# A decoder layer on one Trainium2 core: the last two tiles written out as one ordered piece, routers in pairs, contexts loaded ahead

## The chip, the cores and the metric

The kernel runs on one core of a Trainium2 chip. The metric is the device time of one execution in microseconds (us), the median of several runs. The core's engines are named as in the profile: PE (TensorE, matmuls; PEld its weight loads), DVE (VectorE), ACT (ScalarE), POOL (GpSimd) and SP (SyncE, which here issues DMAs; ACT issues some too).

## What is computed

One decoder layer in float32 on 32 sequences of 64 tokens, 512 features each, so 2048 tokens or 16 tiles of 128 tokens (two sequences a tile):

```python
x = x + attention(layernorm(x))        # 32 heads of 128, q and k rms-normed
x = x + cross(layernorm(x), ctx)       # per sequence, over features
x = x + experts(layernorm(x))

def cross(up, down):                   # up: 64 x 512, down: 64 x 128
    q, k, v = Wq @ up, Wk @ down, Wv @ down
    return Wskip @ up + (softmax(q.T @ k / 8) @ v.T).T

def experts(h):                        # 64 experts, the best 8 of each token
    s = softmax(h @ router.T + router_bias)
    w = s where s is among the token's 8 largest, else 0
    return h * sum(w) + w @ expert_bias
```

The change concerns only the second and the third line.

## The kernel before

**Stages.** Until about 1396 us the kernel does the self-attention of all 16 tiles. Then comes the output stage: the output projection, a 2048 by 4096 by 512 product by Strassen's scheme with seven products for each pair of tiles (`strassen_out`, line 974 and after; `chunks`, matmuls on L879). When a tile's sum with the residual is whole, `done(t, x)` starts its tail: the generator `after_attention`, which does the cross attention and then the experts. Each `yield n` in it gives PE back to the projection: the main loop (end of `decoder_layer`) calls `advance()` after every four matmuls of a product, and `n` is how many calls the tail sits out. So the tails of pair p run between the products of pair p+1, and the tails of the last pair (tiles 14 and 15) have little or nothing to hide behind.

**What sets the order.** PE's order is the program's (`manual_schedule` for PE in the whole kernel). In the output stage the other engines' orders are chosen by the framework's scheduler, which follows the dependences and the buffers; each engine then runs its list strictly in order. Buffers come from pools: PSUM has three banks `ps_s` (kv, energies, logits), two `ps_t` (transposes), three `ps_a` (projection, mixtures, experts). DMAs of a queue are issued in order; each also waits on one of eight semaphores, dealt out in turn among all queues, until the DMA that had it before has landed.

**Cross attention of a tile** (L1084 to L1158). The context `ct` (128x128) is loaded on SP's queue (L1090) when the tail starts. Layernorm: statistics on DVE, `rstd` on POOL (L259, L260) or, in tiles with `name.endswith("15")`, on ACT (L262, L263), the normalising on DVE (L269). `kv`: two matmuls (L1094, L1095), copied by ACT (L1098). Energies `e`: eight matmuls on 64 rows each (L1105). The skip product `py_x` (L1114); softmax on DVE and ACT (L1123 to L1139); eight transposes `pt_x` (L279), two ACT copies `att` (L1144); the mixture of two matmuls on 64 columns each into `py_x` (L1149); the sum on DVE (L1158).

**Experts of a tile** (L1162 to L1226). Layernorm again, four transposes `pt_f` (L279), ACT copy `ft` (L1168), router `pl_f`: four matmuls with `ft` as weights and the router's 64 columns moving (L1173). Bias, the eight largest, softmax, mask and share `wds` on DVE and ACT (L1178 to L1205). The shares are transposed (`pw_f`, L1212) and copied (L1214), for two tiles at once up to tile 13, and each tile's product with the experts' biases (`pm_f`, 512 columns, L1222) is added (L1225) and stored (L1226, 256 KB).

**Fillers.** At the end, where PE has gaps, `fill_behind` puts dummy transposes (`fill`, L230) after named steps of tiles 14 and 15, 76 in all.

Of the kernel before, what the change touches and what calls it, by code (L numbers as in the profile page):

```python
# [13 lines left out]
P = 128  # L14
# [21 lines left out]
def _bc(ap, n):  # L36

    return ap.unsqueeze(2).to_broadcast([ap.shape[0], ap.shape[1], n])
# [3 lines left out]
def decoder_layer(  # L42
# [172 lines left out]
    def load(to, what):  # L215

        tc.keep_in_program_order(nc.sync.dma_start(out=to, in_=what))
# [7 lines left out]
    def fill(count):  # L225
# [3 lines left out]
        for _ in range(count):  # L229
            nc.tensor.transpose(filled[0], ident, ident)  # L230


    FILL = {
        (NT - 1, "keys"): 18,
        (NT - 2, "mixtures"): 18,
        (NT - 1, "probabilities"): 6,
        (NT - 2, "router's input"): 5,
        (NT - 2, "router"): 10,
        (NT - 1, "router's input"): 5,
        (NT - 1, "router"): 3,  # L240
        (NT - 2, "weights"): 3,
        (NT - 2, "experts"): 8,
    }

    def fill_behind(t, what):
        if (t, what) in FILL:
            fill(FILL[t, what])

    def statistics(xs, name, on_gpsimd=False):

        n = len(xs)
# [12 lines left out]
        return [(mv[:, i, 0:1], rstd[:, i : i + 1]) for i in range(n)]  # L264

    def layernorm(xt, name):
        ((mean, rstd),) = statistics([xt], name, not name.endswith(str(NT - 1)))
        xn = work.tile([P, D], F32, tag="xn", name=f"xn_{name}", bufs=3)
        nc.vector.tensor_scalar(xn, xt, mean, rstd, ALU.subtract, ALU.mult)  # L269
        return xn  # L270
# [810 lines left out]
        done(ta, xa)  # L1081
        done(tb, xb)

    def cross_attention(t, xt, apart):  # L1084

        name = f"x{t}"
        ct = work.tile([P, MCTX], F32, tag="ct", name=f"ct_{t}")
        nc.sync.dma_start(out=ct, in_=ctx_flat[bass.ts(t, P), :])  # L1090
        xn = layernorm(xt, name)
        yield 1
        kv = ps_s.tile([P, 2, MCTX], F32, tag="ps", name=f"kv_{t}")
        nc.tensor.matmul(kv[:, 0, :], wqk, ct, start=True, stop=True)  # L1094
        nc.tensor.matmul(kv[:, 1, :], ct, xw[:, 2, :], start=True, stop=True)  # L1095

        kvs = work.tile([P, 2, MCTX], F32, tag="kvs", name=f"kvs_{t}")
        nc.scalar.copy(kvs, kv)  # L1098
        fill_behind(t, "keys")
        yield apart  # L1100
        halves = [slice(b * SEQ, (b + 1) * SEQ) for b in range(2)]
        e = [ps_s.tile([P, 4, MCTX], F32, tag="ps", name=f"e{b}_{name}") for b in range(2)]
        for c in range(4):
            for b, half in enumerate(halves):
                nc.tensor.matmul(  # L1105
# [3 lines left out]
                    start=True,  # L1109
                    stop=True,  # L1110
                )
        def skip():
            py = ps_a.tile([P, D], F32, tag="pa", name=f"py_{name}")
            nc.tensor.matmul(py, xw[:, 3, :], xn, start=True, stop=False, skip_group_check=True)  # L1114
            return py


        py = skip() if t == NT - 1 else None
        probs = []
        for b in range(2):  # L1120

            mx = small.tile([P, 4], F32, tag="mx4", name=f"mx{b}_{name}")
            nc.vector.tensor_reduce(mx, e[b], AX.X, ALU.max)  # L1123
            neg = small.tile([P, 4], F32, tag="neg4", name=f"neg{b}_{name}")
            nc.vector.tensor_scalar(neg, mx, -(SEQ**-0.5), None, ALU.mult)
            prob = work.tile([P, 4, P], F32, tag="probx", name=f"prob{b}_{name}", bufs=3)
            sums = small.tile([P, 4], F32, tag="sums4", name=f"sums{b}_{name}")
            for c in range(4):
                nc.scalar.activation(
                    prob[:, c, :],  # L1130
                    e[b][:, c, :],
                    AF.Exp,
                    bias=neg[:, c : c + 1],
                    scale=SEQ**-0.5,
                    accum_out=sums[:, c : c + 1],
                )
            inv = small.tile([P, 4], F32, tag="inv4", name=f"inv{b}_{name}")
            nc.vector.reciprocal(inv, sums)
            nc.vector.tensor_tensor(prob, prob, _bc(inv, P), ALU.mult)  # L1139
            probs.append(prob)  # L1140
        yield 5
        att = work.tile([P, 2, 4, P], F32, tag="att", name=f"att_{name}", bufs=1)
        for b in range(2):
            nc.scalar.copy(att[:, b, :, :], transposed(probs[b], f"{name}_{b}"))  # L1144
        fill_behind(t, "probabilities")
        yield 2
        py = py or skip()
        for b, half in enumerate(halves):
            nc.tensor.matmul(  # L1149
                py[half, :],  # L1150
                kvs[:, 1, half],
                att[:, b, :, :].rearrange("m c n -> m (c n)"),
                start=False,
                stop=b == 1,
                skip_group_check=True,
            )
        fill_behind(t, "mixtures")
        nc.vector.tensor_tensor(xt, xt, py, ALU.add)  # L1158

    chosen_by = {}  # L1160

    def experts(t, xt):  # L1162
        name = f"f{t}"
        xn = layernorm(xt, name)

        yield 8 if t == NT - 2 else 3
        ft = work.tile([P, KC, P], F32, tag="ft", name=f"ft_{name}", bufs=1)
        nc.scalar.copy(ft, transposed(xn.rearrange("p (kc k) -> p kc k", k=P), name))  # L1168
        fill_behind(t, "router's input")
        yield 1  # L1170
        pl = ps_s.tile([P, NEXP], F32, tag="ps", name=f"pl_{name}")
        for kc in range(KC):
            nc.tensor.matmul(  # L1173
                pl, ft[:, kc, :], rwt[:, kc, :], start=kc == 0, stop=kc == KC - 1
            )
        fill_behind(t, "router")
        lg = work.tile([P, NEXP], F32, tag="lg", name=f"lg_{name}")
        nc.vector.tensor_tensor(lg, pl, rb_b, ALU.add)  # L1178
        top = small.tile([P, 8], F32, tag="top", name=f"top_{name}")
        nc.vector.max(top, lg)  # L1180
        neg = small.tile([P, 1], F32, tag="neg", name=f"neg_{name}")
        nc.vector.tensor_scalar(neg, top[:, 0:1], -1.0, None, ALU.mult)
        ex = work.tile([P, NEXP], F32, tag="ex", name=f"ex_{name}")
        den = small.tile([P, 1], F32, tag="den", name=f"den_{name}")
        nc.scalar.activation(ex, lg, AF.Exp, bias=neg, accum_out=den)
        inv = small.tile([P, 1], F32, tag="inv1", name=f"inv1_{name}")
        nc.vector.reciprocal(inv, den)

        rest = work.tile([P, NEXP], F32, tag="rest", name=f"rest_{name}")
        nc.vector.match_replace(rest, top, lg, -3e38)  # L1190
        chosen = work.tile([P, NEXP], F32, tag="chosen", name=f"chosen_{name}")
        nc.vector.tensor_tensor(chosen, lg, rest, ALU.not_equal)

        alone = t >= NT - 2
        side = 0 if alone else t % 2
        if side:
            wds, other = chosen_by.pop(t - 1)
        else:
            wds = work.tile([P, 2, NEXP], F32, tag="wds", name=f"wds_{name}")
        wd = wds[:, side, :]  # L1200
        nc.vector.scalar_tensor_tensor(wd, ex, inv, chosen, ALU.mult, ALU.mult)
        ws = small.tile([P, 1], F32, tag="ws", name=f"ws_{name}")
        nc.vector.tensor_reduce(ws, wd, AX.X, ALU.add)

        nc.vector.scalar_tensor_tensor(xt, xn, ws, xt, ALU.mult, ALU.add)  # L1205
        if not alone and not side:
            chosen_by[t] = wds, xt
            return
        yield 3
        n = NEXP if alone else 2 * NEXP  # L1210
        pw = ps_t.tile([P, P], F32, tag="pt", name=f"pw_{name}")
        nc.tensor.transpose(pw[0:n, :], wds.rearrange("p a e -> p (a e)")[:, 0:n], ident)  # L1212
        wt = work.tile([P, P], F32, tag="wt", name=f"wt_{name}")
        nc.scalar.copy(wt[0:n, :], pw[0:n, :])  # L1214
        fill_behind(t, "weights")
        yield 1

        both = [(t, xt)] if alone else [(t - 1, other), (t, xt)]
        pms = [ps_a.tile([P, D], F32, tag="pa", name=f"pm{i}_{name}") for i in range(len(both))]
        for i, pm in enumerate(pms):  # L1220
            rows = slice(i * NEXP, (i + 1) * NEXP)
            nc.tensor.matmul(pm, wt[rows, :], eb_sb[rows, :], start=True, stop=True)  # L1222
        fill_behind(t, "experts")
        for (at, it), pm in zip(both, pms):
            nc.vector.tensor_tensor(it, it, pm, ALU.add)  # L1225
            nc.sync.dma_start(out=out_flat[bass.ts(at, P), :], in_=it)  # L1226

    def after_attention(t, xt):
        second = t % 2 and t < NT - 1
        if second:  # L1230
            yield 0
        yield from cross_attention(t, xt, 3 if second else 1)
        yield from experts(t, xt)


    phase = ExitStack()
# [314 lines left out]
    work = ctx.enter_context(tc.tile_pool(name="output", bufs=2, reuse_waits="tile"))  # L1551
    bo_b = work.tile([P, D], F32, tag="bo", name="bo_b", bufs=1)
    load(bo_b, bo.partition_broadcast(P))
    outs = {1: strassen_out(1, right, start_tail, a12)}
    next(outs[1])

# [34 lines left out]
                advance()  # L1591
    while tails:
        advance()


# [49 lines left out]
```

## Time and profile before

| what | us |
|---|---|
| median of 3 runs (lowest, highest) | 1869.87 (1869.63, 1870.72) |
| profiled execution, own time | 1869.75 |
| its span, first to last instruction | 1868.0 |
| granted PE clock over the span | 0.999 |
| PE busy, 1400 to 1480 | 77.07 of 80 |
| PE busy, 1480 to 1780 | 300.00 of 300 |
| PE busy, 1780 to 1841 | 60.36 of 61 |
| PE busy, 1841 to 1868 (fillers included) | 22.30 of 27 |

Times in the trace are counted from the span's first instruction. A line of a timeline has start, duration, engine, line of code, operation, output and inputs, shapes, count, and in brackets the idle time ahead of it with what ended it. A line of waits has the waiting instruction, what it waited for, and the total, number and longest of these waits. A float32 matmul shows as two records (`x2`), a transpose as one. A record's duration reaches beyond the start of the next one, since matmuls are pipelined: what a group costs PE is the distance from its start to the next group's.

### The profile page before, as it was taken

The page shows a single profiled execution, that of the slowest core. Times are in us where ns is not written, and L with a number is a line of the kernel's source. Part 1 is how long each engine was busy: PE and PEld are TensorE (multiplying, and loading weights), DVE is VectorE, ACT ScalarE, POOL GpSimd, SP SyncE. Part 2 cuts the span into 40 slices and gives each one's busy share as a digit, 9 for nine tenths or more (in the row PEclk, how much of TensorE's full clock was granted, in tenths as well). Part 3 has the DMA queues.
Part 4 walks back from the last instruction along what each step waited for, and adds up shares of the span by engine and source line. Part 5 has one row for each costly group of instructions (what it writes and reads, how often), then busy time and mean ns, then how long its engine had stood idle before and what let it go on. Part 6 is the DMA issues. An engine that isn't in the chain of part 4 may idle for free.

```text
span 1868.0 us, 40676 instructions
## 1 busy us (share of the span) xinstructions
PE 1850.4 (99%) x16914; PEld 1616.9 (87%) x16914; DVE 1245.1 (67%) x2110; ACT 653.6 (35%) x1577; POOL 1014.7 (54%) x852
## 2 busy tenths in 40 slices
PE   9999999999999999999999999999999999999999
PEld 8888998898899888898889988988888888788876
DVE  6877777777666758777667767766684445554555
ACT  2344444444433443434443343444312202221222
POOL 4866777776667639776667777766242121212120
PEclk9999999999999999999999999999999999999999
DMA  4234434433443343333343333334944231223100
GB/s 143 69 122 144 134 125 131 131 109 110 131 136 114 114 139 112 109 109 103 130 134 123 109 110 114 103 115 141 312 122 159 91 116 68 71 94 116 46 26 23
DMA packets 164650, 215.06 MB, mean 115 GB/s; under 512 B 10161, under 2 KB 135153, under 8 KB 160369
## 3 DMA queue, kind: packets, MB, share of 16 engines
q1 hardware_dynamic: 157648, 206.62, 34.2%
q10 hardware_dynamic: 6816, 5.83, 1.0%
q8 instruction: 133, 2.18, 0.5%
q14 instruction: 53, 0.43, 0.1%
HBM read 172.05 MB, written 40.37 MB: 114 GB/s over the span
## 4 chain that ended last, share of the span: by engine, by line
PE 88%; DVE 4%; DMA 3%; POOL 3%; ACT 1%; issue 1%; SPq 0%; ACTq 0%; POOLq 0%; DVEq 0%
PE p_w L685 32%; PE py L879 17%; PE va L417 11%; PE vb L417 8%; PE o L622 3%; PE s L585 3%; PE ms_w L821 3%; PE pt_p L279 1%; PE pa L475 1%; PE e_x L1105 1%; PE py_x L1149 1%; PE pt_x L279 1%; POOL w L120 1%; PE pl_f L1173 1%; PE py_x L1114 1%; PE pb L475 1%
## 5 line engine op out<-in xcount | busy, mean ns | idle before, releaser
L685 PE MATMUL p_w<-x,w 128*128 128x256 f32 x2940 | 721.1, 382 | 2.5 <-DVE qk L696 1.7
L685 PEld LDWEIGHTS p_w<-x,w 128*128 128x128 f32 x2940 | 521.4, 190 | 59.3 <-DVE qk L696 1.2
L417 PEld LDWEIGHTS va<-w,x 128*128 128x128 f32 x2048 | 268.6, 192 | 13.0
L696 DVE TENSOR_TENSOR qk<-p_w,qk 128x512 f32<-128x512 f32 x360 | 213.1, 599 | 94.6 <-PE p_w L685 92.3
L433 ACT COPY v<-va 128x256 f32<-128x256 f32 x256 | 96.2, 376 | 497.5 <-PE va L417 497.5
L417 PE MATMUL va<-w,x 128*128 128x128 f32 x2048 | 269.9, 275 | 0.0
L709 DVE TENSOR_TENSOR qk<-p_w,qk 128x512 f32<-128x512 f32 x360 | 220.5, 620 | 46.5 <-PE p_w L685 43.1
L120 POOL TENSOR_TENSOR w<-w 128x768 f32<-128x768 f32 x126 | 249.7, 1993 | 2.4
L572 POOL TENSOR_TENSOR qk<-qk,rs 128x512 f32<-128x512 f32 x128 | 173.0, 1352 | 111.8 <-DMA rs<-row_w 99.4
L295 POOL TENSOR_TENSOR prob<-prob,inv 128x512 f32<-128x512 f32 x64 | 79.2, 1237 | 281.5 <-DVE inv L294 278.3
L879 PE MATMUL py<-wo,a 128*128 128x256 f32 x992 | 227.2, 382 | 0.0
L386 ACT ACTIVATE sq<-qk 128x512 f32<-128x512 f32 x256 | 161.4, 631 | 183.6 <-DVE qk L709 64.4
L879 PEld LDWEIGHTS py<-wo,a 128*128 128x128 f32 x992 | 184.1, 190 | 32.9 <-issue 8.6
L417 PEld LDWEIGHTS vb<-w,x 128*128 128x128 f32 x1536 | 201.3, 192 | 9.7
L417 PE MATMUL vb<-w,x 128*128 128x128 f32 x1536 | 202.4, 275 | 0.0
L574 DVE SCALAR_TENSOR_TENSOR qk<-qk,gqk,rs 128x512 f32<-128x512 f32 x128 | 164.7, 1287 | 3.8 <-DMA rs<-row_w 3.5
L879 PE MATMUL py<-wo_t,a 128*128 128x256 f32 x672 | 155.1, 382 | 0.0
L879 PEld LDWEIGHTS py<-wo_t,a 128*128 128x128 f32 x672 | 124.3, 190 | 18.2 <-issue 1.6
L1003 POOL TENSOR_TENSOR x<-x,p 128x256 f32<-128x256 f32 x42 | 42.9, 1043 | 166.7 <-ACT p L1056 72.2
L437 DVE TENSOR_TENSOR v<-vb,v 128x256 f32<-128x256 f32 x192 | 80.9, 421 | 57.0 <-ACT v L433 28.8
L765 POOL TENSOR_TENSOR qk<-qk 128x256 f32<-128x256 f32 x120 | 102.8, 857 | 10.5 <-DVE qk L709 5.8
L287 DVE TENSOR_REDUCE mx<-s 128x8 f32<-128x512 f32 x64 | 44.1, 689 | 85.4 <-PE s L585 85.3
(197 smaller groups left out, 2253.7 us busy)
## 6 DMA issues: line engine op xcount, KB each, us to landing
rs<-row_w SPq DMA_DIRECT2D x120, 512.0 KB
mixed<-ot SPq DMA_DIRECT2D x64, 512.0 KB
a<-mixed SPq DMA_DIRECT2D x32, 1024.0 KB
w<-in_wq_dram SPq DMA_DIRECT2D x64, 256.0 KB
w<-in_wk_dram SPq DMA_DIRECT2D x62, 256.0 KB
w<-in_wv_dram SPq DMA_DIRECT2D x62, 256.0 KB
x<-in_x_dram SPq DMA_DIRECT2D x20, 256.0 KB
rs<-row SPq DMA_DIRECT2D x8, 512.0 KB
```

The lines of the kernel that those rows point to most:

```text
L120: on.tensor_tensor(*(it.rearrange("p c j d -> p (c j) d") for it in (out, a, b)), ALU.subtract)
L386: nc.scalar.activation(sq, of, AF.Square)
L417: nc.tensor.matmul(to[:, j, :], left[i][:, c, j, :], right[i][:, c, 2, :], start=first and j == 0 and c == 0, stop=c == 1, skip_group_chec ...
L433: nc.scalar.copy(self.v[h, ab], what)
L437: nc.vector.tensor_tensor(it, what, it, ALU.add)
L572: nc.gpsimd.tensor_tensor(k, k, rk, ALU.mult)
L574: lambda: nc.vector.scalar_tensor_tensor(q, q, gqk, rq, ALU.mult, ALU.mult)
L685: nc.tensor.matmul(bank[:, s, :], self.w.inner[o][i], inner_x[self.half, o][i], start=first and s == 0, stop=True, skip_group_check=True,)
L696: nc.vector.tensor_tensor(to(t, j), bank, add(t, j), ALU.add)
L709: nc.vector.tensor_tensor(to(t, j), bank, to(t, j), ALU.add)
L765: on.tensor_tensor(to, to, what, ALU.add)
L879: nc.tensor.matmul(py, a[:, g, :], b[g // KH][:, g % KH, :], start=n == 0 and g == 0, stop=n == last and g == NHG - 1,)
```

## The change

**Contexts.** `context(t)` issues the load; those of tiles 0 and 1 are issued when the output stage's pool opens, ahead of `strassen_out(1, ...)` and so ahead of three of its loads on SP's queue; on that queue these loads now also have other semaphores of the eight.

**Rstd.** `layernorm` takes POOL except for tile 13's cross attention (`name != f"x{NT - 3}"`), which takes ACT.

**Routers in pairs**, tiles 0 to 13. The first tile of a pair only fills its half of `fts`. With the second tile, the router's weights are the stationary side and both tiles' features move, the result being logits by token across; ACT copies it, PE turns it back, and the shares of both tiles are worked out one after the other. The last steps come where they came before.

```diff
+        plt = ps_s.tile([P, P], F32, tag="ps", name=f"plt_{name}")
         for kc in range(KC):
-            nc.tensor.matmul(
-                pl, ft[:, kc, :], rwt[:, kc, :], start=kc == 0, stop=kc == KC - 1
-            )
+            for side in range(2):
+                nc.tensor.matmul(
+                    plt[side * NEXP : (side + 1) * NEXP, :],
+                    rwt[:, kc, :],
+                    fts[:, side, kc, :],
+                    start=kc == 0,
+                    stop=kc == KC - 1,
+                )
+        lgt = work.tile([P, P], F32, tag="wt", name=f"lgt_{name}")
+        nc.scalar.copy(lgt, plt)
+        yield 0
+        pl = ps_s.tile([P, 2, NEXP], F32, tag="ps", name=f"pl_{name}")
+        nc.tensor.transpose(pl.rearrange("p a e -> p (a e)"), lgt, ident)
...
+        for side, (at, x_, xn_) in enumerate(tiles):
...
+        yield 2
```

**The last two tiles.** Tile 14's cross attention stops after its probabilities; tile 15's tail only loads its context. `FILL` goes. When all else is recorded, `last_two()` does the rest of both tiles in one order, given by hand on PE, DVE, ACT and POOL (cut; `normed`, `router`, `shares`, `turned_shares` are as the steps before, except that `shares` leaves the division by `den` to the last addition, and `neg` of the softmax is on ACT):

```diff
+        norm_b, xn_b, *_ = normed(xb, b, False)
+        norm_b()
+        kvs_b = keys(NT - 1, ct_b)
+        py_a = skip(NT - 2, xn_a)
+        mix_in(py_a, kvs_a, att_a)
+        nc.vector.tensor_tensor(xa, xa, py_a, ALU.add)
+        norm_a, xn_a, *_ = normed(xa, f"f{NT - 2}", True)
+        e = energies(NT - 1, xn_b, kvs_b)
+        py_b = skip(NT - 1, xn_b)
+        pc = ps_s.tile([P, NEXP], F32, tag="ps", name="pc")
+        for kc in range(KC):
+            nc.tensor.matmul(pc, mean_of, rwt[:, kc, :], start=kc == 0, stop=kc == KC - 1)
...
+        norm_a()
+        nc.vector.tensor_tensor(
+            centred, rwt, pc.unsqueeze(1).to_broadcast([P, KC, NEXP]), ALU.subtract
+        )
...
+        pt_a = turned_4(xn_a, f"f{NT - 2}")
+        fill(9)
+        probabilities(0)
...
+        nc.vector.tensor_copy(ft_a, pt_a)
+        pl_a = router(ft_a, rwt, f"f{NT - 2}")
+        probabilities(1)
+        lg_a = work.tile([P, 2, NEXP], F32, tag="lg", name=f"lg_{a}")[:, 0, :]
+        nc.vector.tensor_tensor(lg_a, pl_a, rb_b, ALU.add)
+        wd_a, ws_a, inv_a = shares(lg_a, f"f{NT - 2}")
+        fill(6)
+        mix_in(py_b, kvs_b, att_b)
+        nc.vector.tensor_tensor(xb, xb, py_b, ALU.add)
+        wt_a = turned_shares(wd_a, f"f{NT - 2}")
+        fill(5)
+        pt_b = turned_4(xb, f"f{NT - 1}")
...
+        nc.scalar.copy(ft_b, pt_b)
+        norm_b, xn_b, rstd, mean = normed(xb, f"f{NT - 1}", False)
+        nc.vector.scalar_tensor_tensor(xa, xn_a, ws_a, xa, ALU.mult, ALU.add)
+        result(NT - 2, xa, wt_a, inv_a, f"f{NT - 2}")
+        pl_b = router(ft_b, centred, f"f{NT - 1}")
+        lg_b = work.tile([P, 2, NEXP], F32, tag="lg", name=f"lg_{b}")[:, 0, :]
+        nc.vector.scalar_tensor_tensor(lg_b, pl_b, rstd, rb_b, ALU.mult, ALU.add)
+        nc.gpsimd.tensor_scalar(xn_b, xb, mean, rstd, ALU.subtract, ALU.mult)
+        wd_b, ws_b, inv_b = shares(lg_b, f"f{NT - 1}")
+        fill(9)
+        wt_b = turned_shares(wd_b, f"f{NT - 1}")
+        nc.vector.scalar_tensor_tensor(xb, xn_b, ws_b, xb, ALU.mult, ALU.add)
+        fill(2)
+        result(NT - 1, xb, wt_b, inv_b, f"f{NT - 1}")
```

Here `a` is tile 14 and `b` tile 15. Tile 15's router takes the tokens before the normalising: its weights have their mean over the features taken off (`centred`, with `pc` the means by PE), and the logits are scaled by `rstd`, which gives the same logits. `result` does the experts' product, the last addition and the store in two halves of 256 columns, the first half's store on SP's queue and the second's on ACT's:

```diff
+            for part, queue in ((slice(0, D // 2), nc.sync), (slice(D // 2, D), nc.scalar)):
+                nc.vector.scalar_tensor_tensor(
+                    xt[:, part], pm[:, part], inv, xt[:, part], ALU.mult, ALU.add
+                )
+                queue.dma_start(out=out_flat[bass.ts(t, P), part], in_=xt[:, part])
```

## The prediction

> **What bounds the kernel now.** I read the page's busy times and its chain first, then TensorE's waits in the stage that the change touches, then the timelines around each edit.
>
> ```profile
> PE 1850.4 (99%) x16914; PEld 1616.9 (87%) x16914; DVE 1245.1 (67%) x2110; ACT 653.6 (35%) x1577; POOL 1014.7 (54%) x852
> ...
> PE 88%; DVE 4%; DMA 3%; POOL 3%; ACT 1%; issue 1%; SPq 0%; ACTq 0%; POOLq 0%; DVEq 0%
> ```
>
> TensorE (PE) is busy for 99% of the span and holds 88% of the chain that ended last. Until the last matmul of the output projection, whatever is taken off PE, or any wait of PE, shortens the run; work of the other engines there costs nothing. PE's waits from 1396 us, where the output stage begins, to 1841 us are three (total, times, longest):
>
> ```profile
> PE kv L1094 <- DMA ct<-in_ctx_dram: 2.2, 1, 2.2
> PE pm_f L1222 <- DVE x L1225: 0.8, 1, 0.8
> PE e_x L1105 <- ACT prob_x L1129: 0.6, 1, 0.6
> ```
>
> From 1841 us, when the last product is done, to 1868.0 us the span is a chain through all engines: fillers keep PE busy, and a gain there is read from the chain. The kernel has four edits: contexts, paired routers, tile 13's rstd, and the tail. I price each in this order.
>
> **Contexts sooner.** The two ct loads of tiles 0 and 1 stand behind three loads of 1 MB on SP's queue: the first is issued at 1407.61 and lands at 1417.99, and kv starts at 1418.13 after a wait of 2.15. Put ahead of two of these loads and of the second x load, they are issued at about 1397.6 and are there long before 1415.98, when PE arrives. What moves on SP's queue: the first 1 MB load now also waits for the last write of mixed, which lands at 1400.59, so it is issued 3 us later. It stood behind bo_b, which landed by 1402.67, and landed itself at 1405.82; I expect about 1406.3, and PE needs it at 1408.46. If it kept its 8.24 us from issue to landing it would come at 1408.9, a stall of 0.45. The other two are released by small loads that land when they did; x of tile 3 stays behind them, so VectorE's (DVE's) sums stay where they are, and PE, now 2.15 earlier, waits some 0.1 to 0.3 at the transposes of tile 0 (1435.49 before; their second half needs a DVE product that ends at 1433.5). I take **2.0**; bounds 1.3 and 2.15.
>
> **Routers paired** (tiles 0 to 13, seven pairs).
>
> ```profile
> 1442.50 1.08 PE L1149 MATMUL py_x<-att_x,kvs 128*64 128x512 f32 x4
> ...
> 1457.30 1.00 PE L1173 MATMUL pl_f<-rwt,ft_f 128*128 128x64 f32 x8
> 1458.14 1.95 PE L879 MATMUL py<-wo,a 128*128 128x256 f32 x8
> ...
> 1474.44 1.16 PE L1105 MATMUL e_x<-kvs,xn_x 64*128 64x128 f32 x16
> 1475.53 1.99 PE L879 MATMUL py<-wo_t,a 128*128 128x256 f32 x8
> ```
>
> The columns are start, duration, instruction, tile form and count; a float32 matmul is two records. One router now: 1458.14 - 1457.30 = 0.84, and the eight records after it take 1.78 instead of 1.73, so 0.89; a pair 1.78. Its records come every 0.112 though only 64 columns move. After: eight matmuls of 128 moving columns with 64 weights, alternating between the array's two column halves, and one 128x128 transpose (0.11, a quarter of the 0.44 of four). That two halves run together is seen in L1149: its records start in twos, 6 ns apart, and 4 of 512 columns take 1.01 where two of the full array take 0.86. The nearest row for the length is L1105: 16 records of 128 columns in pairs, 1.09, with 0.19 lost around it to the change of form (the products before and after take 0.09 and 0.10 longer). So 1.09 + 0.19 + 0.11 = 1.39, or, with L1149's smaller loss and 8 x 0.12, 1.25. I take 1.33: a gain of 0.45 a pair, **3.15** in all; if the halves ran one after the other (16 x 0.12 + 0.3 = 2.2) it is a loss of 0.43 a pair, 3.0 in all. Bounds -3.0 and 3.7.
>
> What this queues: the new ScalarE (ACT) copy lgt has 1.73 of products as cover and needs about 0.5. DVE now does both tiles' shares between the transpose and pw, with 12 matmuls (5.2) as cover; from the rows of one tile's shares (0.15 to 0.28 each, two ex of 0.54 on ACT) I count 3.6 to 3.8 until wds is whole, in pair 6 (tiles 12 and 13) 5.0 against 5.6 because the normalising of tile 14 stands ahead of it and waits for GpSimd (POOL). So no new wait, with 0.6 to 1.5 to spare. The 0.8 of pm stays: DVE's order there is unchanged.
>
> [...]
>
> **Tile 13's rstd on ACT.** The 0.6 wait of e comes from this:
>
> ```profile
> 1785.88 2.26 DVE L1015 TENSOR_TENSOR a<-a,a_s 128x2048 f32<-128x2048 f32 x1
> 1786.02 1.16 PE L1105 MATMUL e_x<-kvs,xn_x 64*128 64x128 f32 x16
> 1786.05 2.16 POOL L259 TENSOR_SCALAR rs_x<-mv_x 128x1 f32<-128x1 f32 x1 [0.76 <-DVE mv_x L256]
> ```
>
> POOL's one-column operation takes 2.16 beside DVE's sum (median 0.223), so DVE normalises tile 13 at 1788.88, reduces tile 12's energies at 1790.29, and PE waits for PSUM until 1793.62. On ACT it is 0.30 + 0.20, and DVE goes on at 1788.15. If POOL's bias addition then holds DVE up (1.48 instead of 0.546 for L269 before), part of the wait stays. I take **0.5**; bounds 0 and 0.64.
>
> **The tail.** Its lines before:
>
> ```profile
> 1847.33 1.08 PE L1149 MATMUL py_x<-att_x,kvs 128*64 128x512 f32 x4
> ...
> 1848.46 0.69 DVE L1158 TENSOR_TENSOR x<-x,py_x 128x512 f32<-128x512 f32 x1 [1.45 <-PE py_x L1149]
> ...
> 1853.84 0.69 DVE L1158 TENSOR_TENSOR x<-x,py_x 128x512 f32<-128x512 f32 x1 [1.27 <-PE py_x L1149]
> ...
> 1858.58 1.10 PE L1173 MATMUL pl_f<-rwt,ft_f 128*128 128x64 f32 x8
> ...
> 1861.11 0.28 DVE L1201 SCALAR_TENSOR_TENSOR wds_f<-ex_f,inv_f,chosen_f 128x64 f32<-128x64 f32 x1
> ...
> 1862.46 0.27 PE L1212 MATMUL pw_f<-ident,wds_f 128*64 128x128 f32 x1
> ...
> 1863.08 1.12 PE L1222 MATMUL pm_f<-eb_sb,wt_f 64*128 64x512 f32 x2 [0.35 <-ACT wt_f L1214]
> ...
> 1864.24 0.69 DVE L1225 TENSOR_TENSOR x<-x,pm_f 128x512 f32<-128x512 f32 x1 [1.26 <-PE pm_f L1222]
> ```
>
> I follow the new order on the old clock, PE free at 1842.27. (1) Tile 14's skip and mixture come first (0.86 + 0.09 + 1.08): done 1844.30, so e of tile 15 starts there (1844.33 before). DVE does 14's sum and statistics (0.69 + 0.69 + 0.18) before 15's reductions, which start at 1845.95 (1845.52 before). Exponentials 8 x 0.345 with a second neg on ACT between (0.25, estimated from L262 and L263, 0.30 and 0.20): done 1850.1 (1849.9 before). But DVE is free then: prob ends at 1851.0, transposes, copy, mixture, and 15's sum starts at **1853.6** (1853.84 before): 0.24 gained. Tile 14's router lies in the gaps. (2) From that sum to 15's router was 4.74: statistics, rstd, normalising, transposes, copy. The norm now rides on the logits: sum 0.69, transposes 0.14 + 0.63, ACT copy 0.62, which gives 1855.7; but pm of tile 14 is ahead on PE (four records of 0.265, half of L1222's 0.53) until 1856.1. So **2.5**: 2.24 gained. (3) From router to the last addition's end was 6.35 (1858.58 to 1864.93). After: logits +1.19, max, neg, ex, and wds at 1858.9; pw at 1859.06, because 9 fills end at 1858.0, where before 8 fills held it back by 0.96; copy until 1859.62; pm in halves, the last addition 1860.84 to 1861.26. So **5.16**: 1.2 gained. The 3.07 from there to the span's end stay (the output of 256 KB was issued at 1864.96 and landed at 1866.96); halves on two queues may be up to 0.6 shorter, which I don't count. DVE's copy of 14's transposes (0.55 to 0.69, between L269 and L1158) and the centred weights (about 0.42, as L1042) fall in DVE's gaps. Sum **3.7**; bounds 1.0 and 4.2.
>
> **Sum.** 2.0 + 3.15 + 0.5 + 3.7 = 9.35 from the profiled execution's 1869.75 (span 1868.0): 1860.4. The median of the runs, 1869.87, is 0.12 above it: forecast **1860.5**.
>
> **Rivals.**
> *Halves not together:* 6.15 lost against the sum, 1866.7. Against it: the 6 ns in L1149. Chance 0.06.
> *PE's clock falls in the tail*, whose fills shrink from 76 to 31: the granted clock is 0.99 there now with PE busy 22.3 of 27 us; mine has about 16 of 20 and no gap over 1.1. At half speed some 4 us of its matmuls come on top: 1864.5. Chance 0.06.
> *The contexts' wait moves on* to the late 1 MB load or the transposes: 1 to 1.5 back, 1862. Chance 0.12.
> *POOL in the way:* POOL normalises tile 15 from about 1856.3. If it takes 2.9 (its longest 128x512 product, L295) and not 1.25 (L867), DVE's `chosen`, due at 1858.24, waits until 1859.2: 1861.5. The pair of lines at 1786 shows such a hold. Chance 0.10.
> [...]
> *Slower:* pw, in the seven pairs, waits for two tiles' shares. Each wait would have to be over (9.35 + 3.74) / 7 = 1.87, so DVE's chain of 3.8 some 3.3 longer than its cover leaves room for; one POOL addition of 2 us (L1003) in the way isn't enough. At 2.0 each: 1874.5. Chance 0.03.
>
> **How the numbers follow.** The forecast has 0.63 (1859 to 1862.5). 0.2% is 3.74 us, about what a measurement of this kernel can tell from no change: faster below 1866.1, slower above 1873.6. Faster: 0.63 + 0.06 + 0.12 + 0.10 = 0.91, less 0.01 for two rivals at once, 0.90; same 0.07, slower 0.03. All upper bounds together give 1869.75 - 10.7 = 1859.1, with shorter output halves 1858.5: the low end. The high end, 1866.0, takes in the clock and leaves out the halves apart and the slower case.
>
> **What would show it.** kv of tile 0 without a wait and the first 1 MB load landed before PE needs it; eight pairs of L1183 records starting together, about 1.1 long; no wait at pw; no wait at e of tile 13; 15's router 2.5 after its sum, pw right behind wds, the span about 1858.6. Records of L1183 one after the other, a wait of pw on DVE over 0.5, or a granted clock under 0.9 after the last product would make it wrong.

## The result, and the profile after

The changed kernel takes 1859.63 us (median of 5 runs, 1859.22 to 1862.11); five runs of the kernel before have their median at 1869.74. The ratio is 0.9947, with a 95% interval of 0.9936 to 0.9958. The profiled execution of the changed kernel took 1859.63 with a span of 1857.85 by its trace, 10.11 less than the 1867.96 before. The forecast was 1860.5.

Two lines of its page, busy times and the chain by engine:

```profile
PE 1840.6 (99%) x16888; PEld 1606.4 (86%) x16888; DVE 1236.7 (67%) x2106; ACT 654.5 (35%) x1587; POOL 1011.9 (54%) x852
...
PE 92%; DVE 3%; POOL 2%; DMA 1%; issue 0%; ACT 0%; SPq 0%; DVEq 0%; POOLq 0%; ACTq 0%
```

TensorE's share of the chain went from 88 to 92%, but that is no price: four points are some 70 us, seven times the gain. The chain before passed at places through VectorE and GpSimd (from 1775.76 to 1788.22, for one) while TensorE was busy too; the chain after passes through TensorE there. TensorE's own busy time is 9.8 less. TensorE's waits from 1390 us to the end (total, times, longest):

```profile
PE pm_f L1234 <- DVE x L1236: 0.8, 1, 0.8
PE pw_f L1289 <- DVE wds_f L1279: 0.7, 1, 0.7
PE pt_f L262 <- DVE xn_f L1248: 0.4, 1, 0.4
PE pm_f L1298 <- ACT wt_f L1291: 0.2, 1, 0.2
```

The waits of kv and of e are gone, the 0.8 of pm stays, and the other three lie in the tail. Four places of the output stage, in the timeline (start, duration, what):

```profile
1416.13 0.38 PE L1078 MATMUL kv<-ct,wqk 128*128 128x128 f32 x2
...
1460.95 1.09 PE L1183 MATMUL plt_f<-ft_f,rwt 128*64 128x128 f32 x16
1461.97 1.99 PE L862 MATMUL py<-wo,a 128*128 128x256 f32 x8
1463.80 0.27 PE L1194 MATMUL pl_f<-ident,lgt_f 128*128 128x128 f32 x1
...
1781.26 0.29 ACT L245 ACTIVATE rs_x<-mv_x,ln_eps 128x1 f32<-128x1 f32 x1 [1.27 <-DVE mv_x L239]
...
1787.70 1.16 PE L1091 MATMUL e_x<-kvs,xn_x 64*128 64x128 f32 x16
```

kv starts without a wait; sixteen router records take 1.09 where two single routers took 1.00 each; the rstd is on ACT and the sixteen records of tile 13's e run as one. The tail:

```profile
1847.12 0.69 DVE L1371 TENSOR_TENSOR x<-x,py_x 128x512 f32<-128x512 f32 x1
...
1849.51 1.10 PE L1258 MATMUL pl_f<-centred,ft_x 128*128 128x64 f32 x8
1849.73 2.10 POOL L1384 TENSOR_SCALAR xn_f<-x,mv_f,rs_f 128x512 f32<-128x512 f32 x1 [9.15 <-ACT rs_f L246]
...
1851.68 0.23 DVE L1277 TENSOR_TENSOR chosen_f<-lg_x,rest_f 128x64 f32<-128x64 f32 x1
...
1852.29 0.30 PE L1289 MATMUL pw_f<-ident,wds_f 128*64 128x128 f32 x1 [0.69 <-DVE wds_f L1279]
...
1853.00 1.13 PE L1298 MATMUL pm_f<-eb_sb,wt_f 64*128 64x256 f32 x4 [0.19 <-ACT wt_f L1291]
1854.16 0.88 DVE L1302 SCALAR_TENSOR_TENSOR x<-pm_f,inv_f,x 128x256 f32<-128x256 f32 x2 [0.62 <-PE pm_f L1298]
```

Tile 15's router follows its sum by 2.39 (4.74 before), and pw waits for VectorE instead of standing behind fills.

**How the times below are read.** The attention stage, which nothing here touches, ends up to 4.5 us sooner or later from run to run: its last matmul record o starts at 1394.40 in the kernel before, at 1394.72 after, and between 1393.32 and 1397.78 in the experiments. So each profiled run is cut at two records: from the last o to the start of the last record of the output projection (the last *product*; the *stretch*), and from there to the span's end (the *tail*). What stands between two products, their *gap*, is taken from the same records: the start of a product, less the start of the one before, less 0.216, the distance of two products with nothing between them. Spans are taken to two decimals from the traces' first and last instructions.

| run | stretch | tail | span |
|---|---|---|---|
| before | 446.34 | 27.23 | 1867.96 |
| changed | 439.65 | 23.48 | 1857.85 |
| contexts_late | 441.35 | 23.49 | 1861.17 |
| routers_one_half | 445.72 | 23.48 | 1866.46 |
| x13_pool | 440.77 | 23.49 | 1860.35 |
| old_tail | 439.65 | 27.24 | 1861.86 |
| no_fills | 439.65 | 25.14 | 1859.64 |
| pool_longer | 439.65 | 23.51 | 1858.02 |
| pm_apart | 439.95 | 23.09 | 1858.72 |
| pm1_elsewhere | 437.75 | 23.47 | 1854.54 |
| one_piece | 439.65 | 23.71 | 1858.12 |
| routers_single | 443.09 | 23.49 | 1862.50 |
| router15_normed | 441.34 | 27.78 | 1866.90 |
| best | 437.76 | 23.09 | 1857.67 |

Where an edit touches neither, the stretches repeat within 0.01 and the tails within 0.04 (two stretches, told below, do not). The stretch gained 6.69 and the tail 3.75; the attention of the changed kernel's run ended 0.32 later: 6.69 + 3.75 - 0.32 = 10.12.

Each row is one profiled run. Where a run's median is given below, its ratio is to runs of the kernel before from the same session, whose medians were 1872.04, 1871.07 and 1869.59. The intervals of these ratios are wide against the smaller edits, so what an edit is worth is read from the rows above; the medians only bear it out where that is said.

### The profile page after: what moved, and what is told of

Same layout as the page of the kernel before. It is cut to its first block, busy times and chain, and to the rows that moved or that the text cites. A ratio compares the mean times of both kernels' runs of the same rounds, so it can differ in the third digit from the quotient of the medians.

```text
span 1857.8 us, 40650 instructions
## 1 busy us (share of the span) xinstructions
PE 1840.6 (99%) x16888; PEld 1606.4 (86%) x16888; DVE 1236.7 (67%) x2106; ACT 654.5 (35%) x1587; POOL 1011.9 (54%) x852
## 4 chain that ended last, share of the span: by engine, by line
PE 92%; DVE 3%; POOL 2%; DMA 1%; issue 0%; ACT 0%; SPq 0%; DVEq 0%; POOLq 0%; ACTq 0%
PE p_w L668 33%; PE py L862 20%; PE va L400 11%; PE vb L400 9%; PE o L605 4%; PE s L568 3%; PE ms_w L804 3%; PE pt_p L262 1%; PE pa L458 1%; PE e_x L1091 1%; PE py_x L1107 1%; PE pt_x L262 1%; PE py_x L1102 1%; PE pb L458 1%; DVE qk L557 0%; PE pm_f L1234 0%
```

## The experiments

**contexts_late** undoes the sooner contexts:

```diff
-    contexts.update({t: context(t) for t in range(2)})
```

> The changed kernel without the early loads of the contexts of tiles 0 and 1: they are issued behind the three 1 MB loads again. Theory (the queue sets it): kv of tile 0 starts 2.1 to 2.2 after the product before it has ended, and the gap that kv opens between two products, 0.444 without a wait, is about 2.83 as in the kernel before; the whole run is 2.4 longer than the changed kernel, about 1862.0. Rival (part of the gain was given back at the transposes of tile 0, as my forecast has it): kv's gap is the same 2.83, but the run is only 1.8 to 2.1 longer, and the episode of the transposes pt_x of tile 0 is shorter here than in the changed kernel by the difference.

kv waits again, 1.46, and its gap is 2.145 instead of 0.444: 1.70 lost, all of it in the stretch (441.35), while the transposes pt_x with the mixture before them take 2.891 here, before and after alike. So nothing was given back there, and the rival falls. The size missed: 1.70 and not 2.39. Here the last o starts at 1396.34, and TensorE comes to kv 1.94 later than in the kernel before, while the context lands only 1.25 later (1419.24 against 1417.99): the difference is the 0.69 that is missing. So how much this edit saves depends on the end of the attention stage. The runs, 1862.89 and ratio 0.9951 (0.9937 to 0.9965), do not tell this kernel from the changed one (0.9947).

**routers_one_half** takes from the pair only that its tiles work side by side:

```diff
-        plt = ps_s.tile([P, P], F32, tag="ps", name=f"plt_{name}")
-        for kc in range(KC):
-            for side in range(2):
+        plt = ps_s.tile([P, 2, P], F32, tag="ps", name=f"plt_{name}")
+        for side in range(2):
+            for kc in range(KC):
                 nc.tensor.matmul(
-                    plt[side * NEXP : (side + 1) * NEXP, :],
+                    plt[0:NEXP, side, :],
...
-        nc.scalar.copy(lgt, plt)
+        for side in range(2):
+            nc.scalar.copy(lgt[side * NEXP : (side + 1) * NEXP, :], plt[0:NEXP, side, :])
```

> The changed kernel with both tiles of a pair in the same column half: the 8 matmuls of one tile and then the 8 of the other, both into partitions 0 to 63, and two copies instead of one. The same records, the same forms, the same changes of form. Theory (the gain of the paired routers comes from two column halves that work at one time): the 16 records come one after the other every 0.109 to 0.12, an episode costs about 0.9 more than the 1.12 it costs in the changed kernel, 7 pairs 6.0 to 6.5: 1865.7 to 1866.2. Rival (the gain comes from anything else in the pairing: fewer changes of form, the wider moving side): the episode stays within 0.2 of 1.12 and the time within 1.5 of 1859.6.

The first pair in its timeline, the same sixteen records:

```profile
1463.49 1.96 PE L1183 MATMUL plt_f<-ft_f,rwt 128*64 128x128 f32 x16
```

1.96 against 1.09; the gap is 1.984 against 1.117 in all seven pairs, 7 x 0.867 = 6.07, which is the whole of the stretch (445.72 - 439.65). The runs: 1865.5, ratio 0.9976 (0.9964 to 0.9987), clear of the changed kernel's. The gain of the pairing is the two column halves at one time; without it, it would have been a loss.

**routers_single** puts the single routers of before back for tiles 0 to 13.

```diff
-        if t % 2 == 0:
-            fts = work.tile([P, 2, KC, P], F32, tag="att", name=f"ft_{name}", bufs=1)
...
+        ft = work.tile([P, KC, P], F32, tag="ft", name=f"ft_{name}", bufs=1)
```

> The changed kernel with the routers of tiles 0 to 13 each by itself, as in the kernel before; tail, contexts and tile 13 as changed. Theory (the parts add, a pair of routers costs 1.33 and two single ones 1.79): what stands between products in the output stage is 99.1 instead of 95.9, 3.2 more, and the tail is the same 23.45. Rival (the paired routers also moved other waits): the difference is off 3.2 by over 0.4.

The stretch is 3.44 longer. 3.19 of it are the routers: 14 x (0.837 + 0.055) = 12.50 against 7 x (1.117 + 0.104 + 0.109) = 9.31; the other 0.27 is the e of tile 13, which takes 1.452. GpSimd's bias addition (L850, 1788.95 to 1790.22) falls on VectorE's neg (L1133) there, which takes 0.96 instead of 0.16, so the room for e comes later. So beside single routers tile 13's rstd on ScalarE is worth 0.86 (2.308 - 1.452), beside paired ones 1.12. The tail stays.

**x13_pool**:

```diff
-        ((mean, rstd),) = statistics([xt], name, name != f"x{NT - 3}")
+        ((mean, rstd),) = statistics([xt], name, True)
```

> The changed kernel with the rstd of tile 13 on GpSimd again, nothing else. Theory A (a wait row understates what a wait costs, because the two matmuls that could run stretch over the room of sixteen): e of tile 13 costs 2.31 between its two neighbouring products instead of 1.185, so 1.1 are lost, and the wait row of e shows 0.6. Theory B (the wait row is the price): 0.64 lost. Theory C (my forecast): 0.5. GpSimd's one-column operation takes about 2.2 beside VectorE's sum of 2048 columns in all of them; if it takes 0.22, nothing is lost and the cause was another.

From its timeline:

```profile
1782.63 2.16 POOL L242 TENSOR_SCALAR rs_x<-mv_x 128x1 f32<-128x1 f32 x1 [0.76 <-DVE mv_x L239]
...
1789.08 0.49 PE L1091 MATMUL e_x<-kvs,xn_x 64*128 64x128 f32 x2
1790.21 1.16 PE L1091 MATMUL e_x<-kvs,xn_x 64*128 64x128 f32 x14 [0.64 <-ACT prob_x L1137]
```

The wait row says 0.64, the stretch says 1.12, and e's gap 2.308 instead of 1.185 says the same. Theory A holds. Records of the two row halves start 6 ns apart when both may run. Here the first half's two records began at 1789.08 alone, and the other half, which waited for its PSUM, at 1790.21: all the time between the two starts is lost, and the row counts only the part after the first two had ended.

**old_tail** is the kernel before with the other three edits:

```diff
+    contexts.update({t: context(t) for t in range(2)})
...
     def experts(t, xt):
+        if t < NT - 2:
+            yield from experts_of_pair(t, xt)
+            return
```

> The kernel before with the other three edits (contexts sooner, routers of tiles 0 to 13 paired, tile 13's rstd on ScalarE) and with its own old tail: tiles 14 and 15 in their old order with 76 fills, the last router on normed tokens, the output in one piece. Theory (the parts add): 6.7 less than the kernel before, about 1863.1, that is 3.8 more than the changed kernel; from the last product's end to the span's end the same 26.9 as before. Rival (the paired routers or the sooner contexts change what the tail finds: TensorE reaches the end sooner but VectorE's and GpSimd's work on tiles 12 to 14 does not): the stretch from the sum of tile 14 to the end is over 27.5, and the total over 1864.

The stretch is that of the changed kernel, the tail 27.24, that of the kernel before (27.23): the parts add. The runs: 1864.85, ratio 0.9965 (0.9953 to 0.9978).

**no_fills** empties `fill`; no result depends on it.

```diff
-        for _ in range(count):
-            nc.tensor.transpose(filled[0], ident, ident)
+        return
```

> The changed kernel without its 31 fills in the tail. Theory (in this tail the fills keep nothing up: TensorE's work there is short and the granted clock does not follow its gaps within 20 us): the matmuls of the tail keep their durations (the records of the last router every 0.11, the last experts' product 1.13), the stretch from the last product's start to the span's end stays 23.4 to 23.6. Rival (the clock falls without them): the records of the last router come every 0.2 or more, and the stretch is 2 to 5 longer.

My theory falls. The tail is 1.66 longer in the one run taken. By stretches of 4 us, in it and then in the changed kernel (stretch, its length, busy times and counts of PE, PEld, DVE, ACT, POOL, granted clock, DMA share and GB/s):

```profile
1842.00:1846.00 4.00, 2.90 (x19) 2.37 (x17) 3.05 (x10) 2.32 (x12) 0.00 (x0) 0.79 0.00 0
1846.00:1850.00 4.00, 3.45 (x12) 1.41 (x12) 2.58 (x10) 1.40 (x5) 0.00 (x0) 0.79 0.00 0
```

```profile
1842.00:1846.00 4.00, 3.87 (x32) 3.26 (x31) 3.36 (x11) 2.81 (x12) 0.00 (x0) 1.00 0.00 0
1846.00:1850.00 4.00, 4.00 (x22) 2.39 (x23) 2.98 (x9) 1.53 (x6) 0.27 (x1) 1.00 0.00 0
```

The clock falls to 0.79 in both. In the records, the router of tile 14 goes from one every 0.112 to one every 0.213 at 1844.3, in the middle of a run of eight; the clock granted from 1844.30 to 1847.71 is 0.50, then 1.00 again. Ahead of it TensorE was idle for 1.10 (until 1843.21) and some 0.4 more. The two matmul groups that pay, from no_fills' timeline:

```profile
1845.96 2.30 PE L1106 MATMUL py_x<-att_x,kvs 128*64 128x512 f32 x4
...
1854.17 1.75 PE L1297 MATMUL pm_f<-eb_sb,wt_f 64*128 64x256 f32 x4 [0.40 <-ACT wt_f L1290]
```

The mixture takes 2.30 instead of 1.16, so 15's sum comes 1.05 later, and the last product 1.75 instead of 1.13, after an idle 1.68 ahead of pw. The granted clock from 1854 to 1858 is 0.57. So the 31 fills buy 1.66. The falling clock, a rival in the prediction with 0.06, came in this run; in the changed kernel, whose fills stand in these gaps, the clock is 1.00 in both stretches. Idle times of 1.10 and 0.4 stand ahead of the half pace here; in router15_normed, below, 3.42 us of it stand behind a single gap of 0.78.

**pool_longer** doubles GpSimd's work beside the last shares:

```diff
         nc.gpsimd.tensor_scalar(xn_b, xb, mean, rstd, ALU.subtract, ALU.mult)
+        beside = work.tile([P, D], F32, tag="probx", name="beside", bufs=3)
+        nc.gpsimd.tensor_scalar(beside, xn_b, mean, rstd, ALU.subtract, ALU.mult)
```

> The changed kernel with a second GpSimd operation of the same form right behind the normalising of tile 15 (it reads xn_b and writes a tile that nobody reads), so that GpSimd is busy until about 1853.9 of the changed kernel's clock and no longer until 1851.8. Theory (GpSimd does not hold VectorE up here): chosen, wds and the sum with xn_b on VectorE start when they did, relative to the last router, and the stretch from the last product to the span's end stays 23.4 to 23.6. [...]

```profile
1852.08 2.13 POOL L1386 TENSOR_SCALAR beside<-xn_f,mv_f,rs_f 128x512 f32<-128x512 f32 x1
1852.16 0.25 DVE L1279 TENSOR_TENSOR wds_f<-ex_f,chosen_f 128x64 f32<-128x64 f32 x1
...
1853.00 0.75 DVE L1390 SCALAR_TENSOR_TENSOR x<-xn_f,ws_f,x 128x512 f32<-128x512 f32 x1
```

Both of VectorE's operations begin and end inside GpSimd's 2.13 and take 0.25 and 0.75 (0.23 and 0.75 without it); the tail is 23.51. POOL is not in the way here. Had wds waited for the end of GpSimd's operation, it would have started at 1854.2; it starts at 1852.16. Elsewhere in this kernel operations of the two do take longer beside each other. GpSimd's L242 in x13_pool takes 2.16 and ends at 1784.79, VectorE's sum of 2048 columns beside it at 1784.72 (for rs_x, L242 takes 0.21 to 0.23 in the changed kernel). Beside GpSimd's bias addition L850, VectorE's L252 takes 1.48 in x13_pool (0.55 alone) and L1133 takes 0.96 in routers_single (0.16 alone). Beside GpSimd's TENSOR_SCALAR in the changed kernel's tail, VectorE's TENSOR_SCALAR neg_f keeps its 0.15. Which pairs hold each other up stays open.

**pm_apart** gives each half of `result` a PSUM tile of its own:

```diff
-            pm = ps_a.tile([P, D], F32, tag="pa", name=f"pm_{name}")
+            pools = [(ps_a, "pa"), (ps_s, "ps")]
+            pms = [
+                pool.tile([P, D // 2], F32, tag=tag, name=f"pm{i}_{name}")
+                for i, (pool, tag) in enumerate(pools)
+            ]
```

> The changed kernel with the two halves of the last experts' product (tiles 14 and 15) in two PSUM tiles instead of two halves of one. Theory (only the last of the four matmul records signals, so the first half's addition waits for both): with two tiles the first addition starts 0.6 to 0.75 after the product's start instead of 1.16, the second follows at about 1.16, and the last addition ends 0.35 to 0.45 sooner: 23.0 to 23.2 from the last product to the span's end. Rival (the addition waits for TensorE's pipeline or for PSUM's port as long as the other half is written): the first addition begins at 1.16 as before, nothing gained.

```profile
1854.27 1.13 PE L1303 MATMUL pm_f<-eb_sb,wt_f 64*128 64x256 f32 x4 [0.18 <-ACT wt_f L1291]
1855.00 0.92 DVE L1307 SCALAR_TENSOR_TENSOR x<-pm_f,inv_f,x 128x256 f32<-128x256 f32 x2 [0.19 <-PE pm_f L1303]
```

The first addition starts 0.73 after the product (1.16 in the changed kernel), the last ends 0.39 sooner, and the tail is 23.09, 0.39 less. (The stretch is 0.30 longer in this run, which the edit does not touch. It is lost where the first 1 MB load is needed: issued at 1402.64, behind mixed's last write at 1402.62, it lands at 1409.84, and the product that takes it starts at 1409.97 instead of 1409.75, with 0.08 more lost at the next. So the stall that the prediction allowed for behind the sooner contexts is real; in the changed kernel's run the load lands at 1407.14, ahead of its product at 1408.78.) In the changed kernel's trace only the last of the four matmul records raises the semaphore on which the first addition waits.

**one_piece** writes tile 15's end in one piece on one queue:

```diff
+            if t == NT - 1:
+                parts = [(slice(0, D), nc.sync)]
```

> The changed kernel with tile 15's last experts' product, last addition and output in one piece again, stored by one queue. Theory (the halves of the changed kernel gain nothing on the engines, because the first half's addition waits for both; only the smaller transfers gain): the addition starts 1.16 after the product, takes 0.69 and ends 0.2 sooner than the second half does now; the store of 256 KB takes 2.0 from issue to landing instead of 1.75: the stretch from the last product to the end is 23.45 to 23.55, the same within 0.1. Rival (halves on two queues are worth what the transfer shows): 0.25 to 0.6 longer.

The addition takes 0.75 and ends 0.13 sooner than the second half did; but its 256 KB land 2.06 after their issue (1854.98 to 1857.04), the second half's 128 KB after 1.75 (1855.07 to 1856.82). The tail is 0.23 longer, more than the 0.1 of the theory and just under the rival's lower end. The halves are worth 0.23 here: the smaller transfer gives 0.31 and the later addition takes 0.13 back.

**router15_normed** takes back the router on tokens not normed:

```diff
+        norm_b()
         result(NT - 2, xa, wt_a, inv_a, f"f{NT - 2}")
-        pt_b = turned_4(xb, f"f{NT - 1}")
+        pt_b = turned_4(xn_b, f"f{NT - 1}")
...
-        pl_b = router(ft_b, centred, f"f{NT - 1}")
+        pl_b = router(ft_b, rwt, f"f{NT - 1}")
```

> The changed kernel with tile 15's router on normed tokens again: VectorE normalises the tile after its rstd, then the transposes, the copy and the router with the plain weights; GpSimd does nothing there. Theory (statistics, rstd and normalising stand on the path): from 15's sum to its router 4.1 to 4.2 instead of 2.39, the stretch from the last product to the end 1.7 to 1.8 longer, 25.2. Rival (the experts' product of tile 14, which stands ahead of the router on TensorE, hides most of the normalising): under 1.0 longer.

From its timeline:

```profile
1854.87 0.63 PE L262 MATMUL pt_f<-ident,xn_f 128*128 128x128 f32 x4 [1.19 <-DVE xn_f L1248]
1856.59 1.97 PE L1258 MATMUL pl_f<-rwt,ft_x 128*128 128x64 f32 x8 [1.10 <-ACT ft_x L1381]
```

Worse than either theory: the router starts 4.71 after the sum (2.39 changed, 4.1 to 4.2 expected), and the tail is 4.30 longer. 2.32 of that is the later router, a part of it because ScalarE's copy ft_x (1855.95) stood behind the issue of tile 14's second store (1855.54, 0.38) on the same engine. The rest is the clock again: TensorE stood idle for 1.19 and 1.10 where this order has no fills, the router takes 1.97 instead of 1.10, and the clock granted from 1856 to 1860 is 0.58. So this run does not give the price of the normalising alone; an order with fills in these places was not tried. Its stretch is 1.7 longer by another such dip, which the edit does not touch: the clock is 0.50 from 1481.14 to 1484.56, in the middle of products (0.97 over the 50 us from 1450). Ahead of it stands pm's wait of the first pair, 0.78, between matmuls on 64 of the array's rows. The same wait stands in eleven other profiled runs without a dip; what brings the dip in this one is not shown.

**pm1_elsewhere** goes after the 0.8 that the prediction let stand. In the first pair the two products of the experts, which run side by side in the other pairs, go one after the other in the changed kernel's timeline:

```profile
1474.93 1.12 PE L1234 MATMUL pm_f<-eb_sb,wt_f 64*128 64x512 f32 x2
...
1476.84 1.12 PE L1234 MATMUL pm_f<-eb_sb,wt_f 64*128 64x512 f32 x2 [0.78 <-DVE x L1236]
```

```diff
-        pms = [ps_a.tile([P, D], F32, tag="pa", name=f"pm{i}_{name}") for i in range(len(tiles))]
+        pools = [(ps_a, "pa"), (ps_t, "pt") if t == 1 else (ps_a, "pa")]
```

> The changed kernel with the experts' product of tile 1 in a PSUM tile of the transposes' pool instead of the third buffer of the products' pool. Theory (the wait of pm in the first pair is a wait for a PSUM buffer: one is held by a product of the next pair whose sum waits for the x load, one is in use, and the third must first be read by the addition of tile 0): the pm episode of the first pair takes 1.15 between its neighbours instead of 3.05, and 1.9 are gained on TensorE: 1857.7. Rival A (the wait row's 0.8 is the price): 0.8 gained. Rival B (the wait moves on to the transposes or to the product that follows): the sum of all that stands between products in the output stage falls by less than 0.5.

```profile
1473.53 1.13 PE L1238 MATMUL pm_f<-eb_sb,wt_f 64*128 64x512 f32 x4
```

Four records in 1.13; the gap is 1.152 instead of 3.049, the stretch 437.75, 1.90 less. As with e, the row falls short of the price, here 0.8 of 1.90. The runs: 1859.15, ratio 0.9937 (0.9921 to 0.9954), which does not tell it from the changed kernel.

**best** is pm1_elsewhere and pm_apart together.

> The changed kernel with both of the edits that gained: tile 1's experts' product in the transposes' PSUM pool, and the halves of the last two experts' products in PSUM tiles of their own. Theory (the two lie in different stretches and add): what stands between products in the output stage is 94.0 instead of 95.9, the stretch from the last product to the span's end 23.05 instead of 23.45; 2.3 less than the changed kernel, about 1857.3, and 0.9935 of the kernel before. Rival (tile 1's earlier addition and store move the loads behind them, and PE waits elsewhere): what stands between products is over 94.5.

Stretch 437.76 (1.89 less), tail 23.09 (0.39 less): they add in the trace. The runs, 1859.14 and 0.9939 (0.9926 to 0.9951), do not tell it from the changed kernel, nor the expected 1857.3 from 1859.6: the end of the attention stage, 2.1 later in its profiled run, is as large as the gain.

## Why the prediction was right, step by step

The forecast's mechanism held in all four edits; its sizes, on the stretch and the tail:

| term | forecast (bounds) | measured |
|---|---|---|
| contexts | 2.0 (1.3, 2.15) | 2.39 |
| routers | 3.15 (-3.0, 3.7) | 3.19 |
| tile 13 | 0.5 (0, 0.64) | 1.12 |
| tail | 3.7 (1.0, 4.2) | 3.75 |
| sum | 9.35 | 10.45 |

*Contexts*: the step that mis-sized it is the loss I allowed at pt_x. There is none (2.891 in every run), and the late 1 MB load stopped nothing in the changed kernel's run (0.30 in pm_apart's). And the wait row was short: kv's gap fell from 2.834 to 0.444, which is 2.39 where the row had 2.15, because the row begins at the modelled end of the product before, later than where the next record could have started. My upper bound was therefore no bound. In contexts_late the same edit is worth 1.70, inside it: the 2.39 is the value for this end of the attention stage.

*Routers*: a pair costs 1.117 + 0.104 + 0.109 = 1.33, the value chosen, and it rests on the column halves, as routers_one_half shows (2.20 with the 0.21 that follow, where the rival had 2.2). No wait came at the seven pw.

*Tile 13*: the size failed, by the wait row again: 0.64 was its price, and my upper bound, to me; to TensorE it was 1.12. No hold by GpSimd's bias addition came, since it started only at 1783.63.

*The tail*, from the last product: (1) 15's sum 0.36 sooner (0.24 forecast); (2) sum to router 2.39 (2.5); (3) router to the last addition's end 5.53 (5.16), where I let the first half's addition begin after its own half of the product: it waits for both, and pm_apart, with 5.14, gives the forecast's figure; (4) from there to the end 2.81 instead of 3.03, which I had named and not counted. The 0.37 that (3) fell short came back as 0.12, 0.11 and 0.22 in the others, so the tail's nearness to 3.7 is in part luck.

*Sum*: 10.45 against 9.35; 0.32 of it was taken by the later end of the attention, so the time came out 0.9 below the forecast. Two under-priced waits make up most of the difference, and the time itself is near by some luck too: between profiled runs the attention's end moves by up to 4.5. Of the rivals, the halves apart, the contexts' wait moving on (but for pm_apart's 0.30) and POOL in the way did not come; GpSimd's operation took 2.10, between my 1.25 and 2.9, and nobody waited. The falling clock did not come either (1.00 from 1842 to 1854); in the tails of no_fills and router15_normed it did, at 0.50. A case that I had left out is the pm of the first pair: I took its 0.8 as fixed and small, and it was 1.9.

## What to carry to other kernels

Price a wait by the starts of records: the gap between the neighbours that always stand there, less the same gap without the wait. A row of waits understated it here where matmuls overlap or run side by side in parts of the array (0.64 for 1.12, 0.8 for 1.90, 2.15 for 2.39). In this tail, with other engines on the path, an order for TensorE was only as good as its fills: gaps of 1.10 and 0.4 (no_fills) and of 1.19 and 1.10 (router15_normed), and in one run's stretch a single one of 0.78, were followed by a granted clock of 0.50, so each gap has to be looked at before something is moved. And halving an operation paid here by what each half stored (0.23) and signalled (0.39) by itself.

## What had not been expected of the hardware

- In no_fills, gaps in TensorE's work of 1.10 and some 0.4 were followed by 3.41 us at a granted clock of 0.50 (records every 0.213 instead of 0.112), beginning in the middle of a run of matmuls; in router15_normed's stretch a single gap of 0.78 was followed by 3.42 us at 0.50.
- Two VectorE operations with SBUF inputs ran beside a GpSimd operation of 2.13 in 0.25 and 0.75 (pool_longer; 0.23 and 0.75 without it); a one-column operation of GpSimd took 2.16 beside VectorE's sum of 2048 columns (x13_pool), and a four-column TENSOR_SCALAR of VectorE 0.96 beside GpSimd's sum of two tiles (routers_single; 0.16 alone).
- A float32 TENSOR_SCALAR of 128x512 with two column operands took GpSimd 2.10 in the changed kernel, against 1.28 for its sum of two such tiles (L850).
- 256 KB landed 2.06 after their issue (one_piece), 128 KB 1.75 (the changed kernel).
- The attention stage ended at different times, 4.5 us apart, while untouched stretches after it repeated within 0.01 and untouched tails within 0.04.
